# Two edits in a fused layer stack: GpSimd adds pairs of scan products ahead of TensorE, and the routing weights come from a mask

## The chip, the cores and the metric

The kernel runs on one core of one Trainium2 chip, as a single launch. The metric is the device time in microseconds (us) of that core. The kernel before was run three times: 2131.37, 2130.96 and 2122.72 us, median 2130.96 us. A fourth execution was profiled and took 2123.81 us.

The engines are named as the profile names them: PE (TensorE matmuls), PEld (its weight loads), DVE (VectorE), ACT (ScalarE), POOL (GpSimd), SP (SyncE, which only issues DMAs here).

## The reference, cut to what matters

Four layers are applied to `x` (4 batches, 512 tokens, 512 features), each with a residual: an int8-like quantized expert layer, a feed-forward layer whose weights are looked up in a 16-entry table, a selective state-space scan, and a mixture of 32 experts with 8 experts for each token. The change touches the third and the fourth.

```python
    def step(state, inp):                       # third layer: 512 steps in time
        d, b, c, u = inp
        dA = jnp.exp(d[..., None] * A)
        state = state * dA + (d * u)[..., None] * b[:, None, :]
        y = jnp.einsum('bdn,bn->bd', state, c)  # sum over the 16 states n
        return (state, y)
...
    probs = jax.nn.softmax(x @ gate_w, axis=-1) # fourth layer
    w, sel = jax.lax.top_k(probs, K)            # K = 8 of 32
    w = w / jnp.sum(w, axis=-1, keepdims=True)
```

For each of 4 batches, 512 channels and 16 states the scan runs a first-order recurrence over 512 time steps; the 16 states, each multiplied by its row of `c`, are summed into `y`. In the fourth layer each token's eight largest probabilities, divided by their sum, are the weights of its eight experts.

## The kernel before, in words

All of it is written in a tile language: the program's order and each tile's buffer counts are given to a scheduler, which fixes the order of the instructions on each engine's queue. Each queue then runs in that order, and an instruction that waits holds back all that stand behind it on its engine.

The work goes in five parts, by the profile's time: the quantized layer and the building of the looked-up weights (0 to about 324 us); the feed-forward layer of batch 0 up to the first scan (to 420); the middle, where four scans, one for each batch, are woven with the feed-forward layer and with the routing of the batch before (420 to 1235); the gate and the routing of the last batch with the first eight experts (to about 1390); the remaining experts (to the end).

**The middle.** `tile_kernel` weaves, for each batch `b`, the generator `scan(b)`, a slice of `lut_ffn` and, from batch 1 on, `route(b-1)`; `gate(b-1)` runs ahead of them. A call of `scan` has a set-up and 64 units. The set-up is a projection, a convolution of four taps (L433 to L449), `x_proj` (L454), and the step sizes `dt` and the product `dtu = dt*u` (L464 to L477; the last is one POOL instruction of 128 x 2048 elements). A unit is one state `n` (of 16) for one block `e` of 128 channels. Blocks go two at a time (`width` is 2, the number of `py` banks): 16 states for blocks 0 and 1, then 16 states for blocks 2 and 3. In each unit:

- ACT writes `st = exp(A*dt)` into one of two PSUM banks (L490),
- POOL writes `dBu = dtu * B` (L492; three buffers, tag `dBu`),
- DVE runs the recurrence over time in place in `st` (L493),
- DVE writes `sc = st * C` (L495; three buffers, tag `sc`),
- PE adds `sc` into the PSUM bank `py[e]` by a matmul with the identity (L496, in f32; the profile shows two records for each).

`B` and `C` of a state come as one tile `bc`, broadcast to 128 partitions by a DMA of SP's queue (L487; three buffers, so the load for state `n+3` waits until both blocks of state `n` are done with theirs). After 16 states `u` takes up the sum of the block (L499).

**Routing.** `route` (L587) takes layernorm and logits of a batch, softmax (L622 to L627), the eight largest of each token (L631, L632), and their sum's reciprocal `m` (L633, L634). L635 scales the eight values. `one_hot` (L656) makes a 128 x 1024 tile, one row of 32 for each token and choice. L644 multiplies it by the scaled values into another such tile `ow`, and L647 sums that over the choices: the dense weights `w`, written to DRAM beside each token's row (L650). `place` takes the maximum over choices of the one-hot tile as `mask` (L677), from it the position of each token in its expert's list, and scatters 32 columns of token numbers by indirect DMAs of POOL's queue (L707). The 32 scatters of batch `b-1` stand among the 64 units of scan `b`.

**What sets the order.** Each scan's set-up needs the buffers `u`, `sz` and `dt` that the gate of the batch before reads, so a stretch of units is followed by a gap without units, and then by the next stretch. There are four stretches and three gaps.

Of the kernel before, what the change touches and what calls it, by code (L numbers as in the profile page):

```python
# [58 lines left out]
class Kernel:  # L59
# [362 lines left out]
    def scan(self, mp, b):  # L422


        nc, t = self.nc, self.t
        conv_b, dt_b, skip = (self.vecs[:, i, :] for i in range(3))
        cT = mp.tile([P, DC // P, S], F32, tag="sz", name="cT", bufs=1)
        nc.sync.dma_start(out=cT, in_=t["ctxT"][b].rearrange("(k p) l -> p k l", p=P))
        u = mp.tile([P, KH, S], F32, tag="u", name="u", bufs=1)
        for e in range(KH):  # L430
            pi = self.bank("d", "pi")
            for k in range(DC // P):
                nc.tensor.matmul(  # L433
                    pi, lhsT=self.in_w[:, k, e * P : (e + 1) * P], rhs=cT[:, k, :], start=k == 0, stop=k == DC // P - 1
                )
            xin = mp.tile([P, S + 3], F32, tag="dBu", name="xin", bufs=3)
            nc.gpsimd.memset(xin[:, :3], 0.0)
            nc.scalar.copy(xin[:, 3:], pi)
            acc = mp.tile([P, S], F32, tag="sc", name="acc", bufs=3)
            nc.scalar.activation(  # L440
                acc, pi, AF.Identity, bias=conv_b[:, e : e + 1], scale=self.conv_w[:, e, 3:4]
            )
            for j in (2, 1, 0):
                nc.vector.scalar_tensor_tensor(
                    acc, xin[:, j : j + S], self.conv_w[:, e, j : j + 1], acc, ALU.mult, ALU.add
                )
            nc.scalar.activation(u[:, e, :], acc, AF.Tanh)
# [26 lines left out]
        nc.scalar.activation(dtu, dtu, AF.Ln, bias=1.0)  # L474
        nc.vector.tensor_tensor(dtu, dtu, lost, ALU.add)
        nc.vector.tensor_tensor(dt, dt, dtu, ALU.add)
        nc.gpsimd.tensor_tensor(dtu, dt, u, ALU.mult)  # L477

        yield
        py = [None] * KH  # L480
        width = self.bufs["y"]
        for e0 in range(0, KH, width):
            for e in range(e0, e0 + width):
                py[e] = self.bank("y", f"py{e}")
            for n in range(NST):
                bc = mp.tile([P, 2, S], F32, tag="bc", name="bc", bufs=3)
                nc.sync.dma_start(out=bc, in_=self.xdbl[b, 1:3, n, :].partition_broadcast(P))  # L487
                for e in range(e0, e0 + width):
                    st = self.bank("d", "st")
                    nc.scalar.activation(st, dt[:, e, :], AF.Exp, scale=self.A[:, e, n : n + 1])  # L490
                    dBu = mp.tile([P, S], F32, tag="dBu", name="dBu", bufs=3)
                    nc.gpsimd.tensor_tensor(dBu, dtu[:, e, :], bc[:, 0, :], ALU.mult)  # L492
                    nc.vector.tensor_tensor_scan(st, st, dBu, 0.0, ALU.mult, ALU.add)  # L493
                    sc = mp.tile([P, S], F32, tag="sc", name="sc", bufs=3)
                    nc.vector.tensor_tensor(sc, st, bc[:, 1, :], ALU.mult)  # L495
                    nc.tensor.matmul(py[e], lhsT=self.ident, rhs=sc, start=n == 0, stop=n == NST - 1)  # L496
                    yield
            for e in range(e0, e0 + width):
                nc.vector.scalar_tensor_tensor(  # L499
                    u[:, e, :], u[:, e, :], skip[:, e : e + 1], py[e], ALU.mult, ALU.add  # L500
                )
        self.scanned = u
# [84 lines left out]
    def route(self, rp, b):  # L587
# [29 lines left out]
        def tl(shape, dtype, name):  # L617
            return rp.tile(shape, dtype, tag=name, name=name, bufs=1)
# [13 lines left out]
            nc.vector.max_index(sel[:, i, :], top[:, i, :], pr[:, i, :])  # L632
        nc.vector.tensor_reduce(m, top, AX.X, ALU.add)  # L633
        nc.vector.reciprocal(m, m)  # L634
        nc.vector.tensor_tensor(top, top, m.unsqueeze(2).to_broadcast([P, TPB, TOPK]), ALU.mult)  # L635
        nc.vector.tensor_copy(self.chosen[:, t0 : t0 + TPB, :], sel)
        yield
        if b == NB // 2:
            nc.vector.memset(self.seen[0][:, :EARLY], 0.0)
        oh = self.one_hot(rp, b)  # L640

        w = tl([P, TPB, NE], F32, "pr")
        ow = tl([P, TPB * TOPK, NE], F32, "ow")
        nc.vector.tensor_tensor(  # L644
            ow, oh, top.rearrange("p i k -> p (i k)").unsqueeze(2).to_broadcast([P, TPB * TOPK, NE]), ALU.mult
        )
        nc.vector.tensor_reduce(w, ow.rearrange("p (i k) e -> p i e k", i=TPB), AX.X, ALU.add)  # L647
        r0 = 1 + t0 * P
        for xln in self.xln[last:]:
            nc.sync.dma_start(out=xln[r0 : r0 + S, HID:].rearrange("(i p) e -> p i e", p=P), in_=w)  # L650
        yield from self.place(rp, b, oh, self.seen[0], self.tables[last], SLOTS, (ROOM[last], SLOTS))

    def one_hot(self, rp, b):
        oh = rp.tile([P, TPB * TOPK, NE], F32, tag="oh", name="oh", bufs=1)
# [6 lines left out]
        )  # L661
        return oh

    def place(self, rp, b, oh, seen, tables, n, room):

# [7 lines left out]
            return rp.tile(shape, dtype, tag=name, name=name, bufs=1)  # L673

        chosen = self.chosen[:, t0 : t0 + TPB, :].rearrange("p i k -> p (i k)")
        mask = tl([P, TPB, NE], BF16, "mask")
        nc.vector.tensor_reduce(mask, oh.rearrange("p (i k) e -> p i e k", i=TPB), AX.X, ALU.max)  # L677


        pp = self.bank("t", "pp")  # L680
# [226 lines left out]
    def in_full(self, rp, ep, tp):  # L907
# [4 lines left out]
        self.clear(zero, self.tables[2], CAP)  # L912
        nc.sync.dma_start(out=self.x, in_=self.kept.rearrange("(i p) d -> p i d", p=P))
        for b in range(NB):
            run(self.place(rp, b, self.one_hot(rp, b), self.seen[1], self.tables[2], CAP, (CAP, CAP)))
        for e0 in range(0, NE, NE // 2):
            rows = self.table_rows(ep, "exT", self.tables[2], CAP, e0, e0 + NE // 2, CAP)
            tok = self.table_sum(rp, rows, e0, e0 + NE // 2, CAP, "f")
# [11 lines left out]
def run(steps):  # L930
    for _ in steps:
        pass
# [139 lines left out]
```

## Time and profile before

| | us |
|---|---|
| three runs | 2131.37, 2130.96, 2122.72 |
| the profiled execution | 2123.81 |
| its span, first to last instruction | 2121.9 |
| PE busy / DVE busy / POOL busy / ACT busy in the span | 1847.6 / 1239.2 / 971.8 / 663.6 |
| stretches of units, first scan (L493) to last product (L495) | 421.7 to 554.9, 621.0 to 780.8, 847.0 to 1010.1, 1075.6 to 1235.4 |
| L496, all 512 records, busy | 267.4 |
| L644 / L647 / L677, each of four | 1.22 / 1.93 / 1.93 |

A group of the profile is a line of the source, an engine, an operation and its tiles (out<-in), with the number of instructions, the busy time, the mean of one in ns, and after the second bar the idle time of the engine just ahead of them with what ended it. A busy PE is not PE at its peak, since matmuls are pipelined. The table of stretches gives busy time by engine in a piece of the span. The chain of waits is the work that ended last, followed back to what released each step.

### The profile page before, as it was taken

What the parts mean: (1) busy time and instruction counts of PE and PEld (TensorE: products, weight loads), DVE (VectorE), ACT (ScalarE), POOL (GpSimd) and SP (SyncE); (2) the same over time, 40 slices, a digit from 0 to 9 for tenths busy, and PEclk for the clock granted to TensorE, in tenths of its full rate; (3) what the DMA queues carried; (4) which work ended last, traced back from release to release, by engine and by line L of the source; (5) the groups of instructions that cost most, each with busy time, mean ns of one, the idle gap of its engine ahead of it and who ended that gap; (6) DMA issues with size and microseconds to landing.
All of it is one profiled execution on the core that took longest, in us unless ns stands there. A gap on an engine that the chain in (4) does not pass through costs nothing.

```text
span 2121.9 us, 23529 instructions
## 1 busy us (share of the span) xinstructions
PE 1847.6 (87%) x8367; PEld 1104.3 (52%) x8377; DVE 1239.2 (58%) x2029; ACT 663.6 (31%) x1251; POOL 971.8 (46%) x841
## 2 busy tenths in 40 slices
PE   4777859998988998898979979779999999999980
PEld 2443437543644655374636545456656566666650
DVE  6788743599988878987899754122222222222241
ACT  1553441433433334333523232112222222222210
POOL 3111001166338742775067756645555555555431
PEclk9899969999999998899999999869999999999995
DMA  8421106045325532452235586558787877777765
GB/s 260 113 98 54 70 8 225 32 129 129 100 62 112 109 84 60 111 107 72 82 71 117 103 226 141 102 144 179 165 171 163 168 174 150 165 158 151 143 129 178
DMA packets 184499, 266.06 MB, mean 125 GB/s; under 512 B 43138, under 2 KB 89698, under 8 KB 184372
## 3 DMA queue, kind: packets, MB, share of 16 engines
q1 hardware_dynamic: 142628, 180.12, 31.0%
q0 software_dynamic: 41744, 84.34, 21.8%
q8 instruction: 68, 1.11, 0.2%
q14 instruction: 59, 0.48, 0.1%
HBM read 203.68 MB, written 69.18 MB: 129 GB/s over the span
## 4 chain that ended last, share of the span: by engine, by line
PE 36%; DMA 9%; DVE 6%; issue 3%; POOL 3%; ACT 1%; SPq 0%; DVEq 0%; POOLq 0%; ACTq 0%
PE pg L841 16%; PE po_e L859 12%; PE pt_g L829 3%; DMA sums<-ey,to 3%; DMA bc<-xdbl 3%; DVE st L493 2%; POOL dBu L492 1%; DMA acc<-sums 1%; POOL table L707 1%; PE pgu L371 1%; DVE sc L495 1%; PE po_f L387 1%; DMA table<-i_tok,to 1%; DMA xg<-xln,tokens 1%; ACT st L490 1%
## 5 line engine op out<-in xcount | busy, mean ns | idle before, releaser
L841 PE MATMUL pg<-exT,egu 128*128 128x288 f32 (+1 forms) x1536 | 397.5, 417 | 0.1
L492 POOL TENSOR_TENSOR dBu<-dtu,bc 128x512 f32<-128x512 f32 x256 | 322.9, 1276 | 150.7 <-DMA bc<-xdbl 100.4
L865 POOL DMA_INDIRECT sums<-ey,to x168 | 260.7, 1552 | 228.4 <-DMA sums<-ey,to 130.5
L841 PEld LDWEIGHTS pg<-exT,egu 128*128 128x128 f32 x1536 | 289.0, 191 | 116.6 <-issue 30.3
L493 DVE TENSOR_TENSOR_SCAN st<-st,dBu 128x512 f32<-128x512 f32 x256 | 308.4, 1222 | 55.8 <-POOL dBu L492 28.8
L859 PE MATMUL po_e<-ed,eh 128*128 128x512 f32 (+1 forms) x672 | 307.5, 605 | 6.9 <-DVE eh L854 3.8
L496 PE MATMUL py<-sc,ident 128*128 128x512 f32 x512 | 267.4, 638 | 47.7 <-DVE sc L495 46.6
L490 ACT ACTIVATE st<-dt,A 128x512 f32<-128x512 f32 x256 | 170.7, 686 | 391.0 <-DVE sc L495 374.2
L816 POOL DMA_INDIRECT xg<-xln,tokens x168 | 163.7, 974 | 162.0 <-PE pt_g L829 107.6
L853 DVE SCALAR_TENSOR_TENSOR eh<-eh,pg 64x288 f32<-64x288 f32 (+3 forms) x128 | 58.9, 460 | 245.3 <-ACT eh L852 245.1
L859 PEld LDWEIGHTS po_e<-ed,eh 128*128 128x128 f32 (+1 forms) x672 | 113.4, 178 | 169.8 <-issue 164.0
L332 PE MATMUL pw<-oh,lut_t 128*32 128x344 bf16 (+1 forms) x2052 | 132.2, 377 | 71.2 <-DVE oh L326 70.8
L371 PE MATMUL pgu<-xT,wg 128*128 128x256 f32 (+1 forms) x704 | 182.3, 396 | 1.4 <-DVE o L238 0.5
L496 PEld LDWEIGHTS py<-sc,ident 128*128 128x128 f32 x512 | 93.8, 198 | 163.8 <-DVE sc L495 113.9
L371 PE MATMUL pgu<-xT,wu 128*128 128x256 f32 (+1 forms) x704 | 178.7, 393 | 0.0
L495 DVE TENSOR_TENSOR sc<-st,bc 128x512 f32<-128x512 f32 x256 | 167.6, 679 | 5.2 <-PE py L496 0.5
L371 PEld LDWEIGHTS pgu<-xT,wg 128*128 128x128 f32 (+1 forms) x704 | 133.9, 195 | 60.4 <-issue 39.9
L862 DVE TENSOR_SCALAR ey<-po_e,gates 128x512 f32<-128x512 f32 x64 | 48.0, 750 | 199.9 <-PE po_e L859 183.0
L387 PE MATMUL po_f<-wd,h 128*128 128x512 f32 (+1 forms) x352 | 163.2, 601 | 0.0
L864 ACT ACTIVATE ey<-po_e,gates 128x512 f32<-128x512 f32 (+1 forms) x104 | 71.3, 685 | 285.5 <-PE po_e L859 203.6
L371 PEld LDWEIGHTS pgu<-xT,wu 128*128 128x128 f32 (+1 forms) x704 | 137.6, 197 | 33.3 <-issue 12.4
L707 POOL DMA_INDIRECT table<-i_tok,to x128 | 126.8, 991 | 34.3 <-issue 24.2
(254 smaller groups left out, 1931.0 us busy)
## 6 DMA issues: line engine op xcount, KB each, us to landing
bc<-xdbl SPq DMA_DIRECT2D x128, 512.0 KB
egu<-in_w_gate SPq DMA_DIRECT2D x40, 384.0 KB
ix<-idx_b SPq DMA_DIRECT2D x16, 688.0 KB
egu<-in_w_up SPq DMA_DIRECT2D x40, 256.0 KB
ed<-in_w_down SPq DMA_DIRECT2D x40, 256.0 KB
sums<-zero SPq DMA_DIRECT2D x2, 4608.0 KB
acc<-sums SPq DMA_DIRECT2D x16, 512.0 KB
xln<-xn_r SPq DMA_DIRECT2D x24, 256.0 KB
```

The lines of the kernel that those rows point to most:

```text
L371: nc.tensor.matmul(pg[:m, j * W : (j + 1) * W], lhsT=w[:, k, c * P : c * P + m], rhs=xT[:, k, :], start=k == 0, stop=k == KH - 1,)
L387: nc.tensor.matmul(po, lhsT=h[:m, c, i * P : (i + 1) * P], rhs=self.wd[:m, c, :], start=c == 0, stop=c == NIC - 1,)
L490: nc.scalar.activation(st, dt[:, e, :], AF.Exp, scale=self.A[:, e, n : n + 1])
L492: nc.gpsimd.tensor_tensor(dBu, dtu[:, e, :], bc[:, 0, :], ALU.mult)
L493: nc.vector.tensor_tensor_scan(st, st, dBu, 0.0, ALU.mult, ALU.add)
L495: nc.vector.tensor_tensor(sc, st, bc[:, 1, :], ALU.mult)
L496: nc.tensor.matmul(py[e], lhsT=self.ident, rhs=sc, start=n == 0, stop=n == NST - 1)
L707: scatter = nc.gpsimd.indirect_dma_start(out=tables[k % len(tables)], out_offset=bass.IndirectOffsetOnAxis(ap=to[:, i, k : k + 1], axis=0) ...
L816: nc.gpsimd.indirect_dma_start(out=xg[:m, :], out_offset=None, in_=xln, in_offset=bass.IndirectOffsetOnAxis(ap=tokens[:m, lo + j, col : co ...
L841: nc.tensor.matmul(pg[i][:, :hs], lhsT=w[:, k, i * P : (i + 1) * P], rhs=xT[:, k, z : z + hs], start=k == 0, stop=k == KH - 1,)
L859: nc.tensor.matmul(po[:m, :], lhsT=h[:, k, b : b + m], rhs=wd[:, k, :], start=k == 0, stop=k == 1)
L865: nc.gpsimd.indirect_dma_start(out=sums[j], out_offset=bass.IndirectOffsetOnAxis(ap=to[:m, lo + j, col : col + 1], axis=0), in_=y[:m, :], ...
```

## The change

In the scan, PE no longer takes every product. The product of an even state is kept. At the next odd state of the same block, POOL adds the kept product to the odd one in place, and PE adds the sum into `py[e]`: 128 matmuls in place of 256, and 128 new POOL instructions of 128 x 512 f32. The tag `sc` gets five buffers for three.

In the routing, the scaling of the eight values (L635), the 128 x 1024 product `ow` (L644) and its sum over the choices (L647) are gone. The mask is taken first, by the same reduction as before in a function of its own, and the weights are the probabilities times the mask times `m`, two DVE instructions of 128 x 128. The fallback `in_full` (for an overflow of the tables) calls the same new function.

```diff
-            acc = mp.tile([P, S], F32, tag="sc", name="acc", bufs=3)
+            acc = mp.tile([P, S], F32, tag="sc", name="acc", bufs=5)
...
-        py = [None] * KH
+        py, even = [None] * KH, [None] * KH
...
-                    sc = mp.tile([P, S], F32, tag="sc", name="sc", bufs=3)
+                    sc = mp.tile([P, S], F32, tag="sc", name="sc", bufs=5)
                     nc.vector.tensor_tensor(sc, st, bc[:, 1, :], ALU.mult)
-                    nc.tensor.matmul(py[e], lhsT=self.ident, rhs=sc, start=n == 0, stop=n == NST - 1)
+                    if n % 2:
+                        nc.gpsimd.tensor_tensor(sc, sc, even[e], ALU.add)
+                        nc.tensor.matmul(py[e], lhsT=self.ident, rhs=sc, start=n == 1, stop=n == NST - 1)
+                    else:
+                        even[e] = sc
                     yield
...
-        nc.vector.tensor_tensor(top, top, m.unsqueeze(2).to_broadcast([P, TPB, TOPK]), ALU.mult)
...
-        w = tl([P, TPB, NE], F32, "pr")
-        ow = tl([P, TPB * TOPK, NE], F32, "ow")
-        nc.vector.tensor_tensor(
-            ow, oh, top.rearrange("p i k -> p (i k)").unsqueeze(2).to_broadcast([P, TPB * TOPK, NE]), ALU.mult
-        )
-        nc.vector.tensor_reduce(w, ow.rearrange("p (i k) e -> p i e k", i=TPB), AX.X, ALU.add)
+        w = tl([P, TPB, NE], F32, "logits")
+        mask = self.mask(rp, oh)
+        nc.vector.tensor_tensor(w, pr, mask, ALU.mult)
+        nc.vector.tensor_tensor(w, w, m.unsqueeze(2).to_broadcast([P, TPB, NE]), ALU.mult)
...
+    def mask(self, rp, oh):
+        m = rp.tile([P, TPB, NE], BF16, tag="mask", name="mask", bufs=1)
+        self.nc.vector.tensor_reduce(m, oh.rearrange("p (i k) e -> p i e k", i=TPB), AX.X, ALU.max)
+        return m
```

In the order that the scheduler makes of the changed kernel, an add stands on POOL's queue two or three `dBu` products behind the unit that it belongs to, and the 32 scatters of a batch stand between them as before.

More of the change, by code (lines that the diff above doesn't have):

```diff
@@ L650, in route @@
             nc.sync.dma_start(out=xln[r0 : r0 + S, HID:].rearrange("(i p) e -> p i e", p=P), in_=w)
-        yield from self.place(rp, b, oh, self.seen[0], self.tables[last], SLOTS, (ROOM[last], SLOTS))
+        yield from self.place(rp, b, oh, mask, self.seen[0], self.tables[last], SLOTS, (ROOM[last], SLOTS))
     def one_hot(self, rp, b):
@@ L662, in one_hot, with place @@
         return oh
-    def place(self, rp, b, oh, seen, tables, n, room):
+    def mask(self, rp, oh):
+        m = rp.tile([P, TPB, NE], BF16, tag="mask", name="mask", bufs=1)
+        self.nc.vector.tensor_reduce(m, oh.rearrange("p (i k) e -> p i e k", i=TPB), AX.X, ALU.max)
+        return m
+    def place(self, rp, b, oh, mask, seen, tables, n, room):
         nc = self.nc
@@ L675, in place @@
         chosen = self.chosen[:, t0 : t0 + TPB, :].rearrange("p i k -> p (i k)")
-        mask = tl([P, TPB, NE], BF16, "mask")
-        nc.vector.tensor_reduce(mask, oh.rearrange("p (i k) e -> p i e k", i=TPB), AX.X, ALU.max)
         pp = self.bank("t", "pp")
@@ L914, in in_full @@
         for b in range(NB):
-            run(self.place(rp, b, self.one_hot(rp, b), self.seen[1], self.tables[2], CAP, (CAP, CAP)))
+            oh = self.one_hot(rp, b)
+            run(self.place(rp, b, oh, self.mask(rp, oh), self.seen[1], self.tables[2], CAP, (CAP, CAP)))
         for e0 in range(0, NE, NE // 2):
```

## The prediction

> **What bounds the kernel now.** I read the page first, for the costliest groups, then busy time by stretch, then the chain of waits in one stretch, then timelines.
>
> ```profile
> L492 POOL TENSOR_TENSOR dBu<-dtu,bc 128x512 f32<-128x512 f32 x256 | 322.9, 1276 | 150.7 <-DMA bc<-xdbl 100.4
> L493 DVE TENSOR_TENSOR_SCAN st<-st,dBu 128x512 f32<-128x512 f32 x256 | 308.4, 1222 | 55.8 <-POOL dBu L492 28.8
> L496 PE MATMUL py<-sc,ident 128*128 128x512 f32 x512 | 267.4, 638 | 47.7 <-DVE sc L495 46.6
> L495 DVE TENSOR_TENSOR sc<-st,bc 128x512 f32<-128x512 f32 x256 | 167.6, 679 | 5.2 <-PE py L496 0.5
> L707 POOL DMA_INDIRECT table<-i_tok,to x128 | 126.8, 991 | 34.3 <-issue 24.2
> ```
>
> A unit costs POOL 1.276 us, DVE 1.222 + 0.679 = 1.901 us, PE two records. Each scatter costs POOL 0.991 us and about 0.21 us of issue ahead of it (24.2 us over the 116 waits that the fuller listing of this group gives). Before the 256 products POOL idles 150.7 us: it is not the bound. Next, busy time by piece (the halves of the first, second and third stretch; times from its first product on):
>
> ```profile
> core 0: us, PE busy (x) PEld busy (x) DVE busy (x) ACT busy (x) POOL busy (x), PEclk, DMA share, GB/s
> 420.40:485.40 65.00, 55.15 (x153) 27.53 (x152) 61.29 (x77) 23.14 (x38) 42.65 (x34) 0.95 0.44 121
> 485.40:554.90 69.50, 62.73 (x166) 28.76 (x166) 66.64 (x81) 28.50 (x42) 39.00 (x34) 1.00 0.44 107
> ...
> 616.20:691.70 75.50, 64.22 (x176) 34.13 (x176) 69.72 (x91) 23.68 (x39) 57.51 (x49) 0.91 0.50 103
> 691.70:780.80 89.10, 87.74 (x298) 54.98 (x297) 72.05 (x98) 30.46 (x51) 56.52 (x52) 1.00 0.46 85
> ...
> 842.10:915.00 72.90, 63.79 (x172) 34.22 (x172) 68.67 (x92) 23.54 (x38) 56.87 (x49) 0.88 0.45 103
> 915.00:1010.10 95.10, 89.17 (x296) 55.28 (x295) 74.14 (x100) 30.27 (x50) 57.10 (x52) 0.98 0.40 83
> ```
>
> The first stretch is DVE's (127.9 of 134.5 us). In the later ones the first half is DVE's (69.7 of 75.5), the second PE's (87.7 of 89.1). POOL is at 56 to 66% in the first stretch and the second halves, at 76 to 78% in the first halves of the later ones. So PE binds about 90 us of each of three stretches, and nowhere else in the scans. The chain of waits in the third stretch shows what stands in for a single bound:
>
> ```profile
> by line: DMA bc<-xdbl 20.5%; DVE st L493 7.9%; issue 6.9%; DMA table<-i_tok,to 6.8%; POOL dBu L492 5.4%; PE pgu L371 4.4%; DVE sc L495 3.6%; PE py L496 2.7%; ACT st L490 2.4%; DVE g L380 1.1%; DVE u L499 0.8%; SPq L728 0.7%; POOL table L707
> ```
>
> The loop is: DVE ends with a `bc` tile, SP reloads it in about 5 us, POOL makes `dBu`, DVE scans. POOL's part of it comes right after the load:
>
> ```profile
> 930.51 1.27 POOL L492 TENSOR_TENSOR dBu<-dtu,bc 128x512 f32<-128x512 f32 x1 [1.66 <-DMA bc<-xdbl]
> 931.94 0.99 POOL L707 DMA_INDIRECT table<-i_tok,to  x1
> 932.96 1.28 POOL L492 TENSOR_TENSOR dBu<-dtu,bc 128x512 f32<-128x512 f32 x1
> 934.85 1.26 POOL L492 TENSOR_TENSOR dBu<-dtu,bc 128x512 f32<-128x512 f32 x1 [0.61 <-DMA bc<-xdbl]
> ```
>
> **What the skill says.** The Trainium skill, GPSIMD Engine Reference, section Elementwise — side-by-side cycle accounting: a two-input f32 operation runs about 1.96 times as long on GpSimd as on VectorE. The trace agrees: 1276 against 679 ns, 1.88 times. The same engine's added adds therefore cost a full `dBu` each. SBUF — State Buffer, section SBUF: two separate sides: a VectorE operation with two SBUF inputs (or in a two-port mode) and a GpSimd one exclude each other for the whole instruction. The trace agrees: while POOL ran `dtu` (611.61 to 616.11) a DVE operation of 32 columns took 4.35 us, and the next, beside a `dBu`, 1.09 us.
>
> ```profile
> 611.80 4.35 DVE L692 TENSOR_SCALAR over<-chosen 128x32 f32<-128x32 f32 x1
> 616.07 0.41 DVE L380 SCALAR_TENSOR_TENSOR g<-g,pgu 128x256 f32<-128x256 f32 x1
> 616.40 1.09 DVE L684 TENSOR_TENSOR seen<-seen,mask 128x32 bf16<-128x32 bf16 x1
> ```
>
> `dBu` itself stays within 1252 to 1308 ns beside the scans and products, which read `st` from PSUM. Perfetto Trace Analysis, Identifying the Most-Contended Engine, calls matmul busy time a bad measure; here four back-to-back L496 records take 1.72 us on the chain, against a mean of 638 ns each.
>
> **PE's saving.** 128 matmuls go, 0.86 us each when back to back (1.72 / 2): 110 us of PE, 27.5 per stretch. In the built order the feed-forward matmuls between the last unit of a stretch and the first of the next stay about as many (31 to 64 L371 and 6 to 22 L387, for 58 and 7), at 0.43 and 0.86 us: 32, 32 and 33 us against 31. So what PE gains within a stretch can't shorten a gap; it shows only where PE bound, the three second halves, and only as far as the next engine allows.
>
> **POOL's cost.** The add's shape is not in the trace before as such; L492 (1276 ns) and the older in-place add L239 (median 1276, up to 1922) bound it: I take 1.276; at 1.37, L239's mean, 3 us more per stretch. A later stretch, from its first `dBu` to its last, holds 64 products, 30 adds and 31 scatters: 64 x 1.276 + 30 x 1.276 + 31 x 0.991 + 31 x 0.21 = 81.7 + 38.3 + 30.7 + 6.5 = 157.2 us. From first scan to last product it is 1.28 less and 1.90 more: 157.8 us if POOL never idles. Now these three take 159.8, 163.2 and 159.8 us (482.8). POOL becomes the bound in all of them, and the sum at no idle is 473.4: a gain of 9.4 us is the most that the whole saving of PE can bring here. At 2.0% idle it is gone.
>
> **The added wait.** An add waits for its unit's L495 on DVE. Behind it in POOL's queue stand the next `dBu` products and scatters; DVE's scans wait for those, PE's `py` for the add. With five `sc` buffers, product k+3 on DVE needs add k done. POOL leads by two or three units, so a DVE that is late by more than about 1 us (from the end of a state's last `dBu` to the one five units on, POOL has 4 products, 2 adds and 2 scatters, 10.0 us, while two scans and two products, 3.8 us, and the reload, 5.2 us, take 9.0) stops POOL, and a bound engine doesn't get that back. POOL's idle ahead of `dBu` is 37.7 us per stretch now (150.7 / 4), all of it free. I take a fifth of it as remaining, 5% of 157.2 (limits 0, since DVE in the first stretch loses hardly anything as a bound, and 12%, a half). Then a stretch is 157.2 x 1.05 + 0.6 = 165.7 and the three 497: **+14 us**.
>
> **First stretch.** POOL gets 94 x 1.276 = 120 us for 133 and isn't the bound, but the built order moves feed-forward work in: 14 pairs of L380 and L381 for 9, 5 x (0.41 + 0.42) = 4.1 us on a full DVE, given back only in stretches that POOL bounds. With a stall of 1 us: **+5** (0 to +12).
>
> **Routing.** L635, L644 and L647 go (0.18 + 1.22 + 1.93 = 3.33 us); two operations of 128 x 128 come, at 0.29 (L627's row): 2.75 us of DVE less in each gap. In gaps 1 and 2 the built order also puts the 4.35 us operation ahead of `dtu`, out of its shadow (-4.2). But it puts L476, which `dtu` waits for, at the end of DVE's part: `dtu` and the first `dBu` (4.5 + 1.28 us) were covered by DVE work (611.5 to 621.0) and now hardly are, and some 4 us of gate and feed-forward work move from stretches into the gaps. I take **0** for the gaps (-9 to +6 together). In the last batch's routing the 2.75 us are hidden: from 1305 to 1383 POOL's scatters and accumulating stores are the chain; uncovered, 3 us. The end of the last stretch holds memsets and gathers ahead of the last four `dBu` now, afterwards behind all of them: -8 for the gate, later gathers for the experts: 0 (-8 to +5).
>
> **Sum.** 14 + 5 + 0 + 0 = +19 on the profiled 2123.8 us, 2143. That execution lies 7 us under the median of the runs; the four executions have a mean of 2127.2, which I take as the base: **2146 us**, +0.7% on 2130.96. What a measurement of this kernel can tell from no change is about 0.5%, 10.7 us: under 2120.3 is faster, over 2141.6 slower.
>
> **Rivals.**
> - *PE's relief counts (faster).* POOL's queue stays full through the three later stretches, below 2% idle; at zero they give -9.4, the first +0, the gaps -9 for the shorter routing. 2127 - 19 = **2108**. For it: PE at 98% of the second halves, POOL at 63% there. Against it: the first halves have POOL at 77% already. Decided by POOL's idle within a stretch.
> - *Saving and cost cancel (no change).* Idle of 2 to 3%, +4, first stretch +4, gaps -5: 2127 + 3 = **2130**. The change as such would then work, with PE idle where it was busy.
> - *DVE and POOL wait for each other in turn (much slower).* 12% idle: 176.7 a stretch, +47, first stretch +12: **2186**. For it: three `dBu` buffers and two `st` banks; against it: the built lead of two or three units.
> - That the change doesn't do what it says is excluded for its instructions, which the built order shows.
>
> **Chances.** Forecast 0.45, faster 0.27, no change 0.23, much slower 0.05. Faster 0.27, within 0.5% 0.23, slower 0.50. Range: down to the faster rival's 2108, up to 9% idle (172 a stretch, +33, with +10 and +6 elsewhere: 2176).
>
> **What would show it.** Right: POOL over 93% busy in the later stretches, PE under 80% in their second halves, L496's busy time halved, first halves longer than 75 us and second halves shorter than 89, with sums of 163 to 170. Adds near 1.28 us. Wrong: stretches under 160 us with POOL full (the first rival), gaps shorter than 62 us, or adds well over 1.4 us.

## The result, and the profile after

The changed kernel takes 2138.55 us (median of seven runs, 2135.94 to 2142.99), the kernel before 2126.55 (seven runs, 2120.07 to 2131.37): a ratio of 1.0057, 95% interval 1.0039 to 1.0075. It is slower by about 12 us where 19 were forecast, on nearly the same base (2127.2 for 2126.55). The profiled execution took 2138.48 us, its span is 2136.6.

First the groups of the changed kernel, as on its page: busy time and mean of one, then the idle time ahead of them and its releasers.

```profile
L492 POOL TENSOR_TENSOR dBu<-dtu,bc 128x512 f32<-128x512 f32 x256 | 321.4, 1274 | 26.3 <-DMA bc<-xdbl 16.4 <-DVE st L493 8.1
L493 DVE TENSOR_TENSOR_SCAN st<-st,dBu 128x512 f32<-128x512 f32 x256 | 309.3, 1221 | 71.4 <-POOL dBu L492 61.5 <-ACT st L490 9.5
L495 DVE TENSOR_TENSOR sc<-st,bc 128x512 f32<-128x512 f32 x256 | 169.1, 679 | 12.4 <-POOL sc L497 8.2 <-PE py L498 0.6
L498 PE MATMUL py<-sc,ident 128*128 128x512 f32 x256 | 167.3, 744 | 151.2 <-POOL sc L497 145.3 <-DVE ln_rs L102 5.3
L497 POOL TENSOR_TENSOR sc<-sc 128x512 f32<-128x512 f32 x128 | 161.5, 1268 | 15.9 <-DVE sc L495 14.2 <-DVE ln_mv L101 0.2
```

The idle time has changed sides. POOL waited 150.7 us ahead of its `dBu` products and now waits 26.3; the scans wait 61.5 us for `dBu` where they waited 28.8; PE, which was busy 267.4 us with `py`, is busy 167.3 (not half: a record now lasts 744 ns in mean, for 638) and waits 145.3 us for the sums. A sum costs 1268 ns.

Busy time by half in the first two of the three later stretches, from the stretch's first product on:

```profile
core 0: us, PE busy (x) PEld busy (x) DVE busy (x) ACT busy (x) POOL busy (x), PEclk, DMA share, GB/s
617.10:695.30 78.20, 56.12 (x167) 34.54 (x165) 59.03 (x76) 22.73 (x39) 71.25 (x60) 0.87 0.44 95
695.30:786.30 91.00, 72.19 (x195) 42.09 (x195) 73.20 (x96) 30.81 (x48) 81.96 (x71) 0.81 0.37 87
843.70:918.60 74.90, 49.98 (x155) 27.88 (x154) 62.30 (x81) 24.02 (x39) 71.10 (x60) 0.95 0.46 99
918.60:1005.50 86.90, 64.21 (x187) 36.60 (x186) 68.33 (x89) 25.05 (x41) 78.72 (x70) 0.90 0.40 92
```

POOL is busy 90 to 95% of each half; PE, which had 98 and 94% of the second halves, has 79 and 74%. DVE has 75 to 83%. So one engine was taken off its limit and another put on it. The chain of waits in the last stretch says the same, first of the changed kernel, then of the kernel before:

```profile
by line: POOL dBu L492 23.4%; POOL sc L497 16.9%; issue 16.0%; POOL table L711 15.1%; DVE st L493 6.6%; DMA bc<-xdbl 6.1%; PE pgu L371 4.8%; DVE sc L495 3.7%; PE py L498 2.6%; POOL ed L795 0.8%; DVE g L380 0.8%; ACT st L490 0.7%; ACT g L379
by line: DVE st L493 18.2%; DMA bc<-xdbl 16.8%; PE po_f L387 11.8%; POOL dBu L492 11.4%; issue 10.7%; DVE sc L495 8.8%; DMA xg<-xln,tokens 5.1%; ACT st L490 4.4%; POOL table L707 3.4%; PE py L496 2.3%; DVE g L380 1.8%; POOL xg L816 0.9%; PO
```

POOL's products, sums and scatters are 55% of it; products and scatters were 15%.

The next table shows where the 14.7 us between the two spans lie; the experiments' own profiled executions stand in it for later use. All is in us. The first and the three later stretches run from the first scan to the last product, and the gaps lie between them. The end has two parts: from the last product to the matmul that counts the overflow (L785 in the changed kernel), called the way to the late experts below, and from there to the end of the span, called the late experts.

| kernel | first | later three (first + second halves) | three gaps | end | span |
|---|---|---|---|---|---|
| before | 133.1 | 482.8 (220.0 + 262.8) | 66.1, 66.2, 65.5 | 168.8 + 717.7 | 2121.9 |
| after | 135.3 | 491.7 (235.9 + 255.8) | 63.0, 59.4, 72.6 | 172.3 + 722.3 | 2136.6 |
| routing alone | 133.1 | 486.0 (222.5 + 263.4) | 62.8, 61.2, 66.8 | 166.0 + 716.4 | 2112.6 |
| half of PE's products, no sums | 129.5 | 412.7 (203.6 + 209.1) | 64.1, 63.7, 72.9 | 178.9 + 715.4 | 2058.6 |
| sums added, PE takes all | 130.0 | 582.1 (249.0 + 333.2) | 68.6, 69.1, 70.2 | 178.0 + 718.4 | 2238.1 |
| pairs in second blocks | 128.7 | 491.5 (216.3 + 275.2) | 66.5, 72.1, 70.4 | 180.9 + 717.3 | 2148.3 |
| after, six buffers | 136.4 | 489.1 (235.2 + 253.8) | 63.5, 74.1, 74.0 | 179.6 + 724.4 | 2161.9 |
| second blocks, six buffers | 128.3 | 480.5 (217.6 + 262.9) | 66.9, 74.1, 74.0 | 185.7 + 724.7 | 2157.9 |
| after, half the scatters | 134.2 | 448.0 (216.4 + 231.5) | 67.9, 59.4, 72.1 | 165.2 + 722.0 | 2089.3 |
| before, half the scatters | 132.9 | 467.9 (216.0 + 252.0) | 66.2, 67.8, 64.4 | 161.0 + 722.9 | 2104.4 |
| second blocks, sums on DVE | 128.7 | 467.9 (212.9 + 255.0) | 66.2, 71.7, 70.2 | 178.6 + 723.2 | 2127.7 |
| bf16 products | 132.1 | 424.1 (198.3 + 225.9) | 66.0, 68.6, 64.6 | 161.0 + 722.5 | 2059.1 |
| after, memsets on DVE | 134.1 | 487.1 (236.9 + 250.2) | 63.0, 59.5, 72.1 | 178.2 + 723.1 | 2137.8 |
| after, last pair plain | 136.2 | 490.0 (234.7 + 255.2) | 62.9, 59.6, 72.5 | 174.5 + 717.5 | 2133.9 |

Against the kernel before, the changed one loses 15.9 us in the first halves of the later stretches and gets 7.0 back in the second halves, loses 2.2 in the first stretch, gains 2.8 in the gaps (with +7.1 in the third) and 1.6 ahead of the first scan, and loses 8.0 at the end. Of these only 3.5 lie ahead of the late experts. The other 4.6 are in them, and that part has two lengths in this table, 715 to 718 and 722 to 725 us, with and without pairs: in the longer ones PE pauses 3.5 to 5.2 us at the first late expert. PE's timeline of the changed kernel shows it at 1420.70:

```profile
1420.24 0.46 PE L833 MATMUL pt_g<-ident,xg 64*128 64x64 f32 x4 [2.10 <-DVE exT L835]
1424.45 4.04 PE L845 MATMUL pg<-exT,egu 128*128 128x288 f32 x8 [3.75 <-issue]
```

The last bracket, issue, means that PE waited for nothing that the profile shows. The cause stays open. The bf16 kernel and the one before with half the scatters have the pause too, and the last kernel of the table has pairs and no pause, so it is not the pairs'. On record it goes with the chip: the experiments ran on two, all seven profiles of the one have the pause and all five of the other have none. The chip of the first two rows is not on record. So a difference of 4 to 7 us in the last column says nothing of a kernel.

### The profile page after: what moved, and what is told of

Read it like the earlier page. It is cut to its first block, busy times and chain, and to the rows that moved or that the text cites. A ratio compares the mean times of both kernels' runs of the same rounds, so it can differ in the third digit from the quotient of the medians.

```text
span 2136.6 us, 23165 instructions
## 1 busy us (share of the span) xinstructions
PE 1765.2 (83%) x8111; PEld 1065.7 (50%) x8121; DVE 1214.7 (57%) x2025; ACT 663.3 (31%) x1251; POOL 1126.3 (53%) x969
## 4 chain that ended last, share of the span: by engine, by line
PE 35%; POOL 6%; DMA 5%; issue 3%; DVE 3%; ACT 1%; SPq 0%; POOLq 0%; another core or an unknown queue 0%; DVEq 0%; ACTq 0%
PE pg L845 17%; PE po_e L863 12%; PE pt_g L833 3%; DMA sums<-ey,to 3%; POOL table L711 2%; POOL dBu L492 2%; POOL sc L497 1%; DMA acc<-sums 1%; PE pgu L371 1%; DVE st L493 1%; DMA bc<-xdbl 0%; PE pl L611 0%; PE pt_u L753 0%; DVE acc L904 0%; PE pi L433 0%
## 5 line engine op out<-in xcount | busy, mean ns | idle before, releaser
L493 DVE TENSOR_TENSOR_SCAN st<-st,dBu 128x512 f32<-128x512 f32 x256 | 309.3, 1221 | 71.4 <-POOL dBu L492 61.5
L492 POOL TENSOR_TENSOR dBu<-dtu,bc 128x512 f32<-128x512 f32 x256 | 321.4, 1274 | 26.3 <-DMA bc<-xdbl 16.4
L498 PE MATMUL py<-sc,ident 128*128 128x512 f32 x256 | 167.3, 744 | 151.2 <-POOL sc L497 145.3
L371 PE MATMUL pgu<-xT,wg 128*128 128x256 f32 (+1 forms) x704 | 191.5, 409 | 6.4 <-DVE h L381 5.6
L371 PE MATMUL pgu<-xT,wu 128*128 128x256 f32 (+1 forms) x704 | 184.9, 399 | 0.0
L371 PEld LDWEIGHTS pgu<-xT,wg 128*128 128x128 f32 (+1 forms) x704 | 141.3, 205 | 63.9 <-issue 31.4
L497 POOL TENSOR_TENSOR sc<-sc 128x512 f32<-128x512 f32 x128 | 161.5, 1268 | 15.9 <-DVE sc L495 14.2
L498 PEld LDWEIGHTS py<-sc,ident 128*128 128x128 f32 x256 | 47.1, 218 | 216.7 <-POOL sc L497 209.5
```

The costliest lines, as they stand in the source:

```text
L371: nc.tensor.matmul(pg[:m, j * W : (j + 1) * W], lhsT=w[:, k, c * P : c * P + m], rhs=xT[:, k, :], start=k == 0, stop=k == KH - 1,)
L497: nc.gpsimd.tensor_tensor(sc, sc, even[e], ALU.add)
```

## The experiments

Theory: the pairs lift PE's limit, which is worth much, but fill GpSimd's queue, which then sets the pace; the routing edit is separate. Rivals: PE's relief is worth little; what costs is buffers held by pairs; what costs is the passage through a queue in order, not its fill.

### The two edits apart

The routing edit of the change with the scan of before (three `sc` buffers, PE takes all 256 products):

```diff
-                    if n % 2:
-                        nc.gpsimd.tensor_tensor(sc, sc, even[e], ALU.add)
-                        nc.tensor.matmul(py[e], lhsT=self.ident, rhs=sc, start=n == 1, stop=n == NST - 1)
-                    else:
-                        even[e] = sc
+                    nc.tensor.matmul(py[e], lhsT=self.ident, rhs=sc, start=n == 0, stop=n == NST - 1)
```

> Only the routing edit (weights from mask and probabilities); the scan as before, with three product buffers. If GpSimd's adds are the loss, this is as fast as before or a little faster: 0 to -9 us, with the three later stretches as before (483 us in sum). If the routing edit is the loss (its order in the gaps), this is slower than before by 8 us or more, like the changed kernel.

Measured: 2119.65 us, ratio 0.9951 (0.9935 to 0.9968). The routing edit alone gains about 10 us; by the table 7.0 in the gaps and 2.8 ahead of the late experts, while the later stretches lose 3.2. The pairs then cost about 19 us by the medians (2138.55 - 2119.65) and about 23 by the two ratios to the kernel before (1.0057 and 0.9951), whose own median was 2.5 us higher beside this run.

### What PE's relief is worth without the price

The changed kernel without the sums: PE takes only the odd states' products, the even states' products go nowhere.

```diff
-                        nc.gpsimd.tensor_tensor(sc, sc, even[e], ALU.add)
                         nc.tensor.matmul(py[e], lhsT=self.ident, rhs=sc, start=n == 1, stop=n == NST - 1)
-                    else:
-                        even[e] = sc
```

> The changed kernel without GpSimd's adds: TensorE takes the odd states' products alone and the even ones are left out of the sum. It shows what TensorE's relief is worth without its price. If GpSimd's queue is the bound of the changed kernel, the later stretches fall from 164 us to what VectorE holds, 145 to 152 us each, and the kernel is 20 to 40 us faster than before. If TensorE did not bind the second halves (the reload of bc or VectorE did), it is within 10 us of before.

Measured: 2066.21 us, ratio 0.9701 (0.9681 to 0.9721). Against the routing alone that is 53 us, more than expected: the later stretches fall from 486.0 to 412.7, in first halves too. The relief is real and large. What follows later from this run: its third gap (72.9) and the way to its late experts (178.9) are as long as those of the changed kernel or longer, though it has not one sum.

### The sums alone

PE takes all 256 products, and POOL adds the odd one into the even one's buffer, which nobody reads afterwards:

```diff
+                    nc.tensor.matmul(py[e], lhsT=self.ident, rhs=sc, start=n == 0, stop=n == NST - 1)
                     if n % 2:
-                        nc.gpsimd.tensor_tensor(sc, sc, even[e], ALU.add)
-                        nc.tensor.matmul(py[e], lhsT=self.ident, rhs=sc, start=n == 1, stop=n == NST - 1)
+                        nc.gpsimd.tensor_tensor(even[e], sc, even[e], ALU.add)
```

> GpSimd makes the 128 adds (into the even product's own buffer, where nobody reads them) and TensorE still takes all 256 products: the price without the relief. If GpSimd's queue is the bound, the later stretches are no shorter than in the changed kernel, 163 to 172 us each, and the kernel is 10 to 35 us slower than before. If the adds cost only because TensorE waits for them, nobody waits here and it is within 6 us of before.

Measured: 2236.0 us, ratio 1.0492 (1.0469 to 1.0514), far beyond what was expected. It is not the pure price it was meant to be: this sum overwrites a tile that PE must have read, so PE's lateness enters POOL's queue. In the second halves no engine is near its limit (POOL about 75 of 110 us, PE about 85). So it can't be read as the price of a sum; that a sum may cost more than its 1.27 us is no more than hinted here.

### Pairs only where PE bound

```diff
-                    if n % 2:
+                    if b == 0 or e0 == 0:
+                        nc.tensor.matmul(py[e], lhsT=self.ident, rhs=sc, start=n == 0, stop=n == NST - 1)
+                    elif n % 2:
```

> Pairs only where TensorE was the bound and GpSimd had room: in the second two blocks of batches 1 to 3; elsewhere TensorE takes every product. If GpSimd's queue decides, the first halves stay at 73 to 76 us, the second halves fall from 89 to 96 us to 80 to 86 us, and the kernel is 10 to 30 us faster than before. If pairing costs by its waits wherever it stands, the second halves stay at 88 us or more, as in the changed kernel, and the kernel is within 6 us of before.

Measured: 2148.72 us, ratio 1.0081 (1.0061 to 1.0102). The theory of a full queue failed here: the second halves grew to 91.9, 93.8 and 89.5 us with POOL at 79 to 84%, PE at 77 to 78% and DVE at 72 to 76%. That is only a part of the loss: of the 36 us between this span and that of the routing alone, 5.5 lie in the later stretches (11.8 more in the second halves, 6.2 less in the first), 18.2 in the gaps and 14.9 on the way to the late experts, while the first stretch is 4.4 shorter. Two groups of this kernel, and one place in its third stretch, POOL's, DVE's and PE's timelines in turn:

```profile
L495 DVE TENSOR_TENSOR sc<-st,bc 128x512 f32<-128x512 f32 x256 | 169.9, 681 | 61.0 <-POOL sc L499 57.2
L371 PE MATMUL pgu<-xT,wg 128*128 128x256 f32 (+1 forms) x704 | 190.3, 411 | 33.8 <-DVE h L381 33.4
```

```profile
954.42 1.26 POOL L492 TENSOR_TENSOR dBu<-dtu,bc 128x512 f32<-128x512 f32 x1
955.84 1.00 POOL L713 DMA_INDIRECT table<-i_tok,to  x1 [0.16 <-issue]
956.87 1.28 POOL L492 TENSOR_TENSOR dBu<-dtu,bc 128x512 f32<-128x512 f32 x1
958.32 0.99 POOL L713 DMA_INDIRECT table<-i_tok,to  x1 [0.17 <-issue]
959.34 1.27 POOL L499 TENSOR_TENSOR sc<-sc 128x512 f32<-128x512 f32 x1
...
955.33 1.22 DVE L493 TENSOR_TENSOR_SCAN st<-st,dBu 128x512 f32<-128x512 f32 x1
960.64 0.69 DVE L495 TENSOR_TENSOR sc<-st,bc 128x512 f32<-128x512 f32 x1 [4.09 <-POOL sc L499]
...
965.39 3.78 PE L371 MATMUL pgu<-xT,wg 128*128 128x256 f32 x8 [6.79 <-DVE h L381]
```

POOL waits for nothing but its own issue in these five lines, yet it works at `dBu` tiles and scatters that nobody needs yet, while the sum stands behind them. DVE has its scan done at 956.55 and waits 4.09 us, because its next product takes the buffer that the sum sets free. Behind that product stand the feed-forward's `g` and `h` on DVE, and a second product that waits 1.53 us for a sum; PE waits 6.79 us for `h`. The sum costs 1.27 us of POOL and several of everybody.

### One buffer more

`sc` gets six buffers, in the changed kernel and in the one with pairs in the second blocks; the routing's row tile gives up its second to make room.

```diff
-                    sc = mp.tile([P, S], F32, tag="sc", name="sc", bufs=5)
+                    sc = mp.tile([P, S], F32, tag="sc", name="sc", bufs=6)
...
-            xn = rp.tile([P, 1, HID], F32, tag="xn", name="xn_r", bufs=2)
+            xn = rp.tile([P, 1, HID], F32, tag="xn", name="xn_r", bufs=1)
```

> The changed kernel with six product buffers for five (the routing's row buffer has one for two to make room). If GpSimd's occupancy alone bounds the later stretches (91 to 95% busy in them), they stay at 486 to 497 us in sum and the time within 6 us of the changed kernel's. If it is the held product buffer (VectorE waits for the add that frees one), VectorE runs on and the sum falls by 10 us or more.

> Pairs in the second halves of batches 1 to 3 only, with six product buffers for five (the routing's row buffer has one for two). With five, VectorE's product waited 20.5 us for the freeing add in the third stretch's second half, and GpSimd was 80% busy there. If the held buffer is the cause, that wait falls below 8 us, the second halves go from 92 to 83 to 86 us and the kernel gains 15 to 25 us on the one with five. If it is something else, they stay within 3 us.

Measured: 2162.95 us, ratio 1.0135 (1.0094 to 1.0176), and 2158.17, ratio 1.0122 (1.0093 to 1.0151). The single row tile is dear by itself: gaps two and three and the way to the late experts grow by 23 and 10 us together, so only the stretches count here. In the changed kernel they stay (489.1 for 491.7): there the held buffer is not the limit. In the other the second halves shrink from 275.2 to 262.9, and products still wait 49.0 us for sums (57.2 before): a buffer helps a late sum a little.

### POOL's queue, shortened

Every second scatter of the table is left out (half of the choices are then missing from the experts' lists), in the changed kernel and in the one before. That takes 16 x (0.991 + 0.21) = 19 us of POOL out of each later stretch and touches PE and DVE little.

```diff
+                if k % 2 and n == SLOTS:
+                    yield
+                    continue
```

> The changed kernel with every second table scatter of the routing left out (16 for 32 each batch; half of the choices are then missing from the experts' lists). GpSimd's queue is 19 us shorter in each later stretch. If GpSimd decides, these fall from 164 to 146 to 152 us each, and the time by 36 to 65 us with what the last batch's scatters give after the scans (some 15 us). If VectorE's dependence on the adds decides regardless of what else GpSimd does, they fall by less than 5 us each.

> The kernel before with every second table scatter left out, as the partner of the run above. GpSimd has room there, so the later stretches stay within 3 us each of 161 (482.8 in sum), and only the part after the scans gains some 10 to 20 us. If scatters cost the scan other than by GpSimd's time (their DMA writes in the way of the bc loads), the stretches fall here too, by 5 us or more each.

Measured: 2089.83 us, ratio 0.9802 (0.9775 to 0.983), and 2107.64, ratio 0.9896 (0.9868 to 0.9924), both against the full kernel before. The later stretches fall by 43.7 us in the changed kernel, by 14.9 in the one before, which was expected to move less. The difference, 29 us of the 58 removed, is what fewer scatters are worth with the pairs and not without. And the sign turns: with half the scatters the kernel with pairs is the faster by 18 us. That is not the routing edit, which differs between the two as well: the later stretches alone are 19.9 us apart, where that edit by itself made them no shorter. So what else POOL's queue holds decides whether the pairs pay. This run doesn't part the queue's fill from a sum's place in it, since with fewer scatters fewer sums stand behind one; the same sums ahead of the scatters were not tried.

### The same pairs without the crossing

The kernel with pairs in the second blocks, with the sum on DVE right behind the odd product:

```diff
-                        nc.gpsimd.tensor_tensor(sc, sc, even[e], ALU.add)
+                        nc.vector.tensor_tensor(sc, sc, even[e], ALU.add)
```

> The kernel of the second blocks alone (pairs only in the second blocks of batches 1 to 3, where PE bound before), with one word changed: the sums of pairs are made by DVE, in place, right behind the odd product, and not by GpSimd. Nothing of a pair crosses engines then, except to PE. PE does 72 us of work there as in that kernel; DVE gets 16 sums of about 0.68 us = 11 us in each second half, on the 68 to 74 us it has. Theory (what the pairs cost there is the passage through GpSimd's queue in order: a sum stands behind products and scatters, the next product of DVE waits for its buffer, and the feed-forward waits behind that): the second halves fall from 92, 94 and 90 us to about 82 to 88, no product waits for a sum, and the time is 2100 to 2125. Rival 1 (the pairs cost because PE gets its work in lumps, two states late, whoever adds): the second halves stay at 90 us or more, 2140 to 2155. Rival 2 (the sums on DVE exclude GpSimd, as both read two operands in SBUF, and its dBu get longer): dBu above 1.4 us in the mean of the second halves and 88 us or more each.

Measured: 2129.13 us, ratio 0.9991 (0.9982 to 1.0001). This kernel's product group, and its sums:

```profile
L495 DVE TENSOR_TENSOR sc<-st,bc 128x512 f32<-128x512 f32 x256 | 169.4, 680 | 5.0
L499 DVE TENSOR_TENSOR sc<-sc 128x512 f32<-128x512 f32 x48 | 53.1, 1107 | 0.5
```

No product waits for a sum, and the second halves are 87.0, 83.4 and 84.6 us, 20.2 less in sum than with the sums on GpSimd, as the theory had it. The sums also leave POOL 61 us of work less (48 x 1.27), but POOL was not full there, and the waits for sums, 57.2 us, are gone: the crossing was the cost there. DVE is the limit now, 84.1 of 87.0 in the first of them. A sum took 1107 ns in mean, 665 at the least and 2511 at the most, where a product that reads `st` from PSUM takes 680: the Trainium skill, SBUF — State Buffer, section SBUF: two separate sides, has a VectorE operation with two SBUF inputs and a GpSimd operation that reads SBUF exclude each other for a whole instruction. The trace agrees: 18 sums began while a `dBu` had 0.20 to 1.26 us to run and no other `dBu` followed in time; each ended 0.55 to 0.56 us after that `dBu`, and the 16 that met no `dBu` took 0.67 to 0.69 us. `dBu` hardly paid (1.29 to 1.31 us in these halves, 1.275 with the routing alone). The time missed the forecast of at most 2125 because gaps two and three and the way to the late experts are 27 us longer than with the routing alone; the late experts, 7 longer, have the pause.

### PE's relief for nothing

The routing edit, no pairs; DVE writes its product as bf16, and PE sums all 256 with the bf16 identity, so the products are rounded to bf16 and summed in f32 as before:

```diff
-                    sc = mp.tile([P, S], F32, tag="sc", name="sc", bufs=5)
+                    sc = mp.tile([P, S], BF16, tag="sc", name="sc", bufs=3)
...
+                    nc.tensor.matmul(py[e], lhsT=self.identb, rhs=sc, start=n == 0, stop=n == NST - 1)
```

> The routing edit of the changed kernel; no pairs; the product that DVE writes is rounded to bf16, and PE sums all 256 with the bf16 identity[...]. GpSimd has no sums, DVE the same instructions. Theory (PE's relief is worth tens of us, and is lost in the changed kernel only because GpSimd pays for it): as the kernel that left out half of PE's products, which ran 2066: 2055 to 2080, the three later stretches 410 to 425 us in sum. Rival (half of the products left out won by something else than PE's time, by fewer hand-overs from DVE to PE or fewer buffers held): 2095 to 2120.

Measured: 2061.16 us, ratio 0.9677 (0.9658 to 0.9696): faster than the kernel before and the changed one, at the price of the rounding. The later stretches take 424.1 us, as the theory had it; as no product is left out here, what was won above was PE's time, and not fewer hand-overs. Its group:

```profile
L496 PE MATMUL py<-sc,identb 128*128 128x512 bf16 x256 | 102.4, 401 | 106.3 <-DVE sc L495 102.2 <-DVE st L493 3.2 <-issue 0.4
L495 DVE TENSOR_TENSOR sc<-st,bc 128x512 bf16<-128x512 f32 x256 | 170.4, 680 | 4.0 <-issue 0.4
```

256 records in place of 512, and DVE's product costs what it did. Where every f32 summand stays f32, the routing alone is the best of these kernels.

### The end

Two variants aim at the 8 us of the end. The first moves the memsets of the experts' buffers from POOL to DVE:

```diff
-            nc.gpsimd.memset(b[: P // 2, 1, :], 0.0)
+            nc.vector.memset(b[: P // 2, 1, :], 0.0)
```

> The changed kernel with the memsets of the experts' buffers on DVE instead of GpSimd, where they stand behind all dBu and the last sums. Theory (the 8 us that the end of the kernel lost come from the gathers that start 22 us later, behind these memsets): first gather earlier by 10 us or more, the end of the kernel shorter by 3 to 8 us, 2130 to 2136. Rival (the last batch's routing sets the end, and its scatters and the copies ahead of them start no earlier): gathers earlier or not, the time from the last product to the end stays within 2 us of 894.5, 2136 to 2141.

Measured: 2144.5 us, ratio 1.0075 (1.0053 to 1.0096); the way to the late experts grew from 172.3 to 178.2 us. The first gather left 8 us earlier (1231.2), but then four gathers stood ahead of the last but one sum, and `u` on DVE waited 6.31 us for `py`. Both expectations fell. The second takes the last sum away, so that PE sums the last two states one by one:

```diff
+                    if b == NB - 1 and e0 and n >= NST - 2:
+                        nc.tensor.matmul(py[e], lhsT=self.ident, rhs=sc, start=False, stop=n == NST - 1)
-                    if n % 2:
+                    elif n % 2:
```

> The changed kernel, only that the last two states of the second block of the last batch are summed by PE one by one, without GpSimd: two sums fewer, two passes of PE more. Background: in the changed kernel the last sum starts 2.9 us after its product, behind a table scatter, the reciprocal root of the layer norm and a gather of the experts; the last py product on PE comes 4.9 us after the last product of DVE (a transposition for the experts ahead of it), the gate's first transposition 12.2 us after it, against 4.3 us in the kernel before. Theory (the 8 us that the end lost hang on the end of the last pair, and so on the queue of GpSimd there): the last py within 2 us of the last product, the gate's first transposition at 5 to 9 us, the end (last product to end of span) 886 to 891 us in place of 894.5, the time 2130 to 2136. Rival (the experts' buffers and gathers, which stay behind all dBu, set the end): py and gate earlier, but the end 892 us or more, the time 2136 to 2142.

Measured: 2135.87 us, ratio 1.0061 (1.0037 to 1.0086). The last `py` came 0.6 us after the last product, but the gate's first transposition still 14 us after it, and the way to the late experts took 174.5 us; the 2.5 us by which the whole end is shorter lie in the pause alone. That is nearer the rival (892 us or more; measured 892.0), though the gate came no earlier. DVE's timeline of this kernel there:

```profile
1241.19 0.69 DVE L495 TENSOR_TENSOR sc<-st,bc 128x512 f32<-128x512 f32 x1
...
1250.03 0.69 DVE L837 COPY exT<-pt_g 128x512 f32<-128x512 f32 x1 [4.73 <-PE pt_g L835]
1250.66 2.29 DVE L518 SCALAR_TENSOR_TENSOR sz<-th,sz 128x2048 f32<-128x2048 f32 x1
```

A copy for the experts, which waits 4.73 us for the transposition of gathered rows, stands ahead of the gate's `sz`, which needs nothing from it. The kernel with half of PE's products, which has no sums, lost more there (178.9). That points to the built order: with pairs the scheduler puts the gate's layer norm and the experts' gathers behind the last unit, and the gate behind the experts' first copies. Which of the two moves weighs more, and whether the pairs or the larger number of `sc` buffers makes the scheduler do so, was not tried.

## Why the prediction was right or wrong

The direction and the mechanism of the stretches held, and the sum came within 8 us. That is in part luck: the scans cost 11 us and not 19, and what was set to nothing, the routing against the gate's later start, was off in opposite directions.

**PE's saving and POOL's cost** held in the main. Sums near 1.28 us: 1.268. PE's busy time for the products fell by 100 us, to 63% and not to half. POOL busy 90 to 95% in the later stretches (over 93 was asked, so this was met only in part), PE under 80%, first halves 80.6, 75.5 and 79.8, second halves 87.3, 84.3 and 84.2. The step *"the sum at no idle is 473.4"* with 5% idle gave +14 us; measured are 491.7, an idle of 3.9% ((491.7 - 473.4) / 473.4) and **+8.9**. So the step was the right one, and only its idle a little too large. One of the three stretches (159.8) and one gap (59.4) fell on the side that was named as speaking against the forecast; the sums of the three did not. The faster rival had its point of decision at 2% of idle, and the idle lay beyond it; the run with fewer scatters shows that the sign can turn. (That rival's own sum is -18.4 and not -19: -9.4, 0 and -9.) One sentence didn't hold: that PE's saving *"shows only where PE bound, the three second halves"*. Without the sums the first halves too fell from 222.5 to 203.6 us.

**The added wait** was in the prediction with its place, but priced only as POOL's idle. The sum's own lateness was not: in the kernel with pairs in the second blocks, DVE and PE wait for a sum behind scatters while POOL is busy all the time. In the changed kernel that wait is small (8.2 us of products waiting for sums); that DVE has little to hurry for where POOL binds may explain it, and is not shown. What was called 5% of idle on a full queue is thus the right size for this kernel alone.

**First stretch**: +5 forecast, +2.2 measured.

**Routing and gaps**: the term *"I take 0 for the gaps"* was mis-sized as a sum of two things. The routing edit by itself gains: gaps -7.0, the way to the late experts -2.8, ratio 0.9951. The pairs then give back in the third gap: 66.8 to 72.6. There the changed kernel shows, POOL's and then DVE's timeline:

```profile
1004.92 1.00 POOL L711 DMA_INDIRECT table<-i_tok,to  x1 [0.16 <-issue]
1005.95 1.04 POOL L103 TENSOR_TENSOR ln_rs<-ln_rs,mhalf 128x4 f32<-128x4 f32 x1
...
1004.79 0.69 DVE L495 TENSOR_TENSOR sc<-st,bc 128x512 f32<-128x512 f32 x1
1007.03 1.28 DVE L105 SCALAR_TENSOR_TENSOR ln_off<-ln_mv,ln_rs 128x4 f32<-128x4 f32 x1 [1.54 <-POOL ln_rs L103]
...
1013.24 2.29 DVE L516 SCALAR_TENSOR_TENSOR sz<-th,sz 128x2048 f32<-128x2048 f32 x1 [4.15 <-ACT th L515]
```

and the kernel before, on DVE:

```profile
1006.92 2.27 DVE L512 SCALAR_TENSOR_TENSOR sz<-th,sz 128x2048 f32<-128x2048 f32 x1
...
1009.43 0.68 DVE L495 TENSOR_TENSOR sc<-st,bc 128x512 f32<-128x512 f32 x1
```

Before, the gate's `sz` was done ahead of the stretch's last product; now it starts 7.8 us after it (1013.24 - 1005.48). The whole layer norm of the gate left the stretch for the gap. The prediction counted "some 4 us of gate and feed-forward work" there and took it as balanced by savings. The run without sums has the same third gap (72.9), which points to the order and not to POOL's load.

**The end**: the step *"-8 for the gate, later gathers for the experts: 0 (-8 to +5)"* failed, by less than the table's +8.0 shows: without the pause in the late experts it is **+3.5** against the kernel before, and +6.3 against the routing alone (172.3 - 166.0). The +3.5 lies within the bounds; the 0 rested on a credit that wasn't there. The credit for memsets and gathers that no longer stand ahead of `dBu` was given to a gate that got nothing from it. In the changed kernel it waits behind those gathers, PE's and then DVE's timeline after the last product, which ends at 1242.08:

```profile
1246.16 1.09 PE L833 MATMUL pt_g<-ident,xg 128*128 128x128 f32 x4 [2.59 <-DMA xg<-xln,tokens]
1247.05 1.91 PE L498 MATMUL py<-sc,ident 128*128 128x512 f32 x2
...
1248.99 0.75 DVE L503 SCALAR_TENSOR_TENSOR u<-u,vecs,py 128x512 f32<-128x512 f32 x1 [4.43 <-PE py L498]
...
1250.45 2.28 DVE L516 SCALAR_TENSOR_TENSOR sz<-th,sz 128x2048 f32<-128x2048 f32 x1
```

The gate's `sz` starts 8.4 us after the last product, where it started 0.6 us after it before (1235.99 and 1235.42).

In sum against the profiled spans: first stretch +2.2, later stretches +8.9, gaps -2.8, end +8.0, ahead of the first scan -1.6: +14.7, where +19 was forecast as 5, 14, 0 and 0. Of the +14.7, the 4.6 in the late experts can't be put down to the change; without them it is +10.1, near the 12.0 between the medians. Against the routing alone, and without the late experts, the pairs cost 18 us of span: 5.7 in the later stretches, 2.2 in the first, 4.2 in the gaps and 6.3 on the way to the late experts. So over half of it lies outside the scans.

## What to carry to other kernels

Moving work from a full engine to a half idle one pays only as far as the receiver's time in that very stage allows: here the 128 products that PE was spared were worth 53 us by themselves, and the 38 us per stretch that they cost POOL, with the order that came with them, took all of it and more. On a queue in order, a short new step costs its place as well as its time: look at what stands ahead of it, and at the buffer that its end sets free. And a change in a loop can move the order of what comes after it, so compare the built order of the stages behind the loop before calling their cost nothing.

## What the runs showed of the hardware

The granted clock did not follow PE's busy share: in the second half of the first later stretch PE was granted 1.00 with the routing alone, busy 97%; 0.81 in the changed kernel, busy 79%, and 0.85 and 0.87 in its last two variants; and 1.00 again with half of its products left out, busy 80%. PE's longest pauses in that half were 1.1 us with the routing alone, 3.1, 2.9 and 2.7 in the changed kernel, and 2.7, 2.4 and 1.8 with half of the products left out. Whether pauses set the clock was not tried.

An f32 matmul of 128 x 512 leaves two records, a bf16 one of the same shape one; the group takes 267.4 us against 102.4 for the same 256 products. DVE's f32 sum of two SBUF tiles took 0.67 to 2.51 us beside GpSimd's own work of that kind, and it was mostly DVE that paid: `dBu` rose from 1.275 to at most 1.31 us in the mean of a half, with single ones up to 2.08.
